# A two-layer graph attention network: sets of seven products that overlap at their ends, and layer 2's gathering one graph later

## The chip, the cores and the metric

The kernel runs on one core of a Trainium2 chip. The metric is the device time of one execution in microseconds (us). TensorE (PE) multiplies, VectorE (DVE) and ScalarE (ACT) do the elementwise work, GpSimd (POOL) issues the accumulating transfers, and SyncE (SP) issues all other DMA transfers. Every engine works through its own instructions in the order in which they stand; engines wait for each other by semaphores.

## The reference

There are 32 graphs of 512 nodes. For each, the input is normalised and rectified, goes through a graph attention layer of 4 heads with 256 features each and an ELU, and then through a second one of 1 head with 512 features; the input is added at the end.

```python
def gat_layer(x, mask, W, a_src, a_dst, bias, concat):
    xl = (x @ W).reshape(B, N, H, F)
    asrc = jnp.einsum('bnhf,hf->bnh', xl, a_src)
    adst = jnp.einsum('bnhf,hf->bnh', xl, a_dst)
    e = jax.nn.leaky_relu(asrc[:, :, None, :] + adst[:, None, :, :], 0.2)
    e = jnp.where(mask[..., None], e, NEG_INF)
    attn = jax.nn.softmax(e, axis=1)
    out = jnp.einsum('bsdh,bshf->bdhf', attn, xl)
    ...
h = jnp.maximum(_layernorm(x, axis=-1), 0.0)
h = jax.nn.elu(gat_layer(h, mask, W1, att_src1, att_dst1, b1, concat=True))
return x + gat_layer(h, mask, W2, att_src2, att_dst2, b2, concat=False)
```

The mask is the adjacency matrix with the diagonal added, and all is fp32.

## The kernel before

**Products.** Most matrix products are cut into 2 x 2 blocks and computed with seven block products in place of eight, with sums of blocks made by DVE beforehand. `sevens` (L866) runs a set of seven for the projections and for layer 2's gathering, `gather1` (L1079) for layer 1's gathering (attention times features), two heads at a time. A product is 8 matmul records for two halves (16 in the second projection). Its sum stands in PSUM. There are four pairs of PSUM banks, given out by `Banks` (L45); a set uses three roles: "a" for products 1, 6, 7 and 4, "b" for 5 and 3, and "g" for 2. Product 1 is copied by ACT from "a" into "g" (the fork), and then 6 goes on accumulating in "a" while 2 goes on in "g". After each product one instruction takes its result out: ACT copies it (`act`, L422) or DVE adds it to what is there (`dve`, L425). So product 6 can start only when the fork copy has read its bank, 7 when the copy of 6 has, and so on; and a new set can start in a bank only when its last result is out. The order of the products is 1, 5, 6, 2, 7, 3, 4 in layer 1's gathering (L1070) and 1, 5, 6, 3, 7, 2, 4 elsewhere (`LAST`, L907). `take2` (L73) gives the free pair to which the narrowest products were last written.

**One graph's turn.** The loop at L1371 runs, on PE and per turn i: gathering of heads 0 and 1 of graph i+1, projection of half the heads of graph i+2, gathering of heads 2 and 3 of graph i+1, projection of the other half of graph i+2, layer 2's gathering of graph i, and the second projection of graph i+1. Each set runs to its end before the next starts. The features of layer 2 stand in one buffer, `xl2`.

**Softmax.** `first` (L710) makes the row sums. For each of four tiles of 128 nodes ACT computes a leaky relu into a buffer `l` (3 of them), DVE adds the mask `mt` and takes the row minimum, and ACT takes the exponential with its sum. Then `spread` (L665) lays the two resulting rows out: DVE transposes them, SP stores them to DRAM (`drr`), and SP loads them broadcast to all partitions (`rr`, two buffers). `second` (L763) makes the attention itself, in buffers `p` (3 of them): DVE combines the row with the column per tile (p<-rr), POOL adds the mask from DRAM by two accumulating transfers (p<-dm), and ACT takes the exponential (p<-p). `columns` (L691) does the same spreading with the row of scores (`das`, `as`).

**Masks and inputs.** `masks` (L555) loads four tiles of the adjacency matrix, makes bf16 masks in `m` (four tiles), stores them to DRAM (`dm`) and has them transposed by two transposing DMAs into `mt`. `norm_turn` (L606) rectifies a tile of x with ACT, stages it as two halves of 16 bit (`adj`<-x), has SP transpose these by DMA (x<-adj, L637), and copies them back into `ht` with ACT. `elu` (L983) uses buffers `xr` (4 of them).

**The order of work.** Every operation is a job with an estimated cost, what it reads and what it writes (`Program`, L87). The PE jobs keep the order in which the program adds them. All other engines' orders are made by a planner (`order`, L234) that simulates the program with its own costs and due times, backwards and forwards, and takes the best of its tries; so a change of a few lines moves instructions on all engines. The whole program has one line per kind of job in the profile: L422 for ACT, L425 for DVE, L428 for SP's transfers, L433 for POOL's, L439 for PE.

Of the kernel before, what the change touches and what calls it, by code (L numbers as in the profile page):

```python
# [44 lines left out]
class Banks:  # L45


    def __init__(self, tiles):
        self.tiles = tiles
        self.free = [(i, j) for i in range(len(tiles)) for j in range(2)]  # L50
        self.written = {q: 512 for q in self.free}

    def take(self, width=512, seeded=0):
        n = [sum(i == k for k, _ in self.free) for i in range(len(self.tiles))]
        fit = [q for q in self.free if self.written[q] >= seeded]
        half = next((q for q in fit if n[q[0]] == 1), fit[0])
        least = min(self.written[q] for q in fit)
        half = next((q for q in fit if self.written[q] == least and n[q[0]] == 1), half)
        self.free.remove(half)
        self.written[half] = max(width, self.written[half] if seeded else 0)  # L60
        i, j = half
        return ("mm", i, j), self.tiles[i][:, j, :]
# [10 lines left out]
    def take2(self, width, seeded=0):  # L73
        whole = [i for i, j in self.free if j == 0 and (i, 1) in self.free]
        least = {i: min(self.written[i, j] for j in range(2)) for i in whole}
        i = min((i for i in whole if least[i] >= seeded), key=least.get)
        self.free = [q for q in self.free if q[0] != i]
        for j in range(2):
            self.written[i, j] = max(width, self.written[i, j] if seeded else 0)
        return [("mm", i, j) for j in range(2)], self.tiles[i]  # L80
# [218 lines left out]
def tile_gat(  # L299
# [79 lines left out]
    xl2 = sbuf.tile([P, NT, DO + 2], F32, name="xl2")  # L379
# [7 lines left out]
    xrs = slots("xr", 4, [P, N])  # L387
    ls = slots("l", 3, [P, N])
    ps_ = slots("p", 3, [P, NT, N])
    m = sbuf.tile([P, NT, N], BF16, name="m")  # L390
# [5 lines left out]
    drs = slots("drr", 2, [2 * NT, P], F32, dram)  # L396
    mds = slots("dm", 3, [P, NT, N], BF16, dram)
    stats = slots("stats", 2, [P, NT, nc.vector.BN_STATS_DIM + nc.vector.BN_AGGR_DIM + 1])
    zs = slots("z", 4, [P, 5, 2, NT])
# [13 lines left out]
    )  # L413

# [140 lines left out]
    def masks(b):  # L555

        for t in range(NT):
            ak, a = adjs.take()
            dma(0.75, (), [ak], a, adj[b, t * P : (t + 1) * P, :])
            dve(  # L560
                0.34, [ak], [("m", t)], nc.vector.tensor_scalar,
                m[:, t, :], a, 0.0, -BIG, op0=OP.is_le, op1=OP.mult,
            )
            adjs.give(ak)
        blocks = bass.AP(tensor=m.tensor, offset=m.offset, ap=[m.ap[0], [N + P, NT], [1, P]])
        every = [("m", t) for t in range(NT)]
        dve(
            0.5, every, every, nc.vector.tensor_max,
            blocks, blocks, diag[:, None, :].to_broadcast([P, NT, P]),
        )  # L570
        MASK[b] = mk, md = mds.take()
        dma(0.45, every, [mk], md.rearrange("p t n -> p (t n)"), m.rearrange("p t n -> p (t n)"))
        tk, mt = mts.take()

        for t in (0, 2):
            prog.add(
                "SP", 1.3, every, [tk + (t // 2,)],
                lambda t=t: nc.sync.dma_start_transpose(
                    mt[:, t : t + 2].rearrange("p t d r -> p (t d) r"),
                    m[:, t : t + 2].rearrange("p t n -> p (t n)"),  # L580
# [76 lines left out]
    class Soft:  # L657
# [7 lines left out]
        def spread(self, v, keys, rows, to, through, n=NT):  # L665

            k = rows * n
            ok, o = to.take()
            dk, dr = through.take()

            c = 32 // k
            sb = o[:, 0, :32]
            dve(
                0.12, keys, [ok], nc.vector.transpose,
                sb, bass.AP(tensor=v.tensor, offset=v.offset, ap=[v.ap[0], [1, k], [0, c]]),
            )
            dma(
                0.03, [ok], [dk], dr[:k].rearrange("k (b j) -> b k j", j=32),
                bass.AP(
                    tensor=sb.tensor, offset=sb.offset, ap=[[c * sb.ap[0][0], P // c], [1, 32]]  # L680
                ),
                0.55,
            )
            dma(
# [6 lines left out]
        def columns(self, i, given=None):  # L691
# [15 lines left out]
                z[:, 0].rearrange("p h t -> p (h t)"), keys, n, ass, das  # L707
            )

        def first(self, h, parts=((0, NT),)):  # L710
# [9 lines left out]
            for d0, d1 in parts:  # L720
# [35 lines left out]
                self.rr[h].append((d0, d1, *self.spread(v, [wk + (2, d0)], 2, rrs, drs, n)))  # L756
# [6 lines left out]
        def second(self, h):  # L763
# [9 lines left out]
            for d0, d1, rk, rr in self.rr.pop(h):  # L773
                at, n, cs = slice(d0 * P, d1 * P), (d1 - d0) * P, range(d0 // 2, d1 // 2)
                long = n == N
                for u in range(NT):
# [7 lines left out]
                    if here:  # L784
                        dve(
                            0.59 if long else 0.34, keys + [("m", u)], keys, nc.vector.tensor_add,
                            p[:, u, at], p[:, u, at], m[:, u, at],
                        )
                rrs.give(rk)
                if not here:  # L790
                    mk, md = MASK[self.b]
                    for us in (0, 1), (2, 3):
                        keys = p_keys(pk, us)
                        accumulate(
                            2.2, keys + [mk], keys,
# [70 lines left out]
    def sevens(left, right, rkeys, put, kh, units, width, order, seeds={}):  # L866
# [3 lines left out]
        for us, n in order:  # L870
            acc, first = ACC[n], n in (1, 5) or n == 2 and us not in forked
            if first:
                seed = seeds.get(n)
                bank[us, acc] = banks.take2(width, 0 if seed is None else M)
# [19 lines left out]
            if n == 1 and banks.able(width):  # L894
                bank[us, "g"] = gks, gt = banks.take2(width, width)
# [11 lines left out]
    LAST = tuple(((0, 1), n) for n in (1, 5, 6, 3, 7, 2, 4))  # L907
    FOUR = LAST + tuple(((2, 3), n) for _, n in LAST)

    PARTS = tuple(((0, 1), n) for n in (1, 2, 5, 6, 3, 7, 4))  # L910
# [4 lines left out]
        (xl2[:, :, :FH], [("xl2", t, 0) for t in range(NT)]),  # L915
        (xl2[:, :, FH + 1 : 2 * FH + 1], [("xl2", t, 1) for t in range(NT)]),
# [45 lines left out]
    def project1(b, left):  # L962
        def to(us, r, c):
# [8 lines left out]
            KQ, [(m, j) for j in range(H // 2) for m in range(2)], W, FOUR,  # L972
# [43 lines left out]
    def sums1(hs_, ps):  # L1016
# [5 lines left out]
        def a_block(i, j):  # L1022
            return (
                xl[:, 2 * j : 2 * j + 2, h0 : h0 + nh, 2 + i * P : 2 + (i + 1) * P],
                [("xl", 2 * j + k, h, i) for k in range(2) for h in hs_],
            )
# [18 lines left out]
        for h, (pk, p) in zip(hs_, ps):  # L1045
# [5 lines left out]
                for r in range(2) for c in range(2)  # L1051
# [18 lines left out]
    PAIRS_OF = tuple(tuple(((h, h + 1), n) for n in (1, 5, 6, 2, 7, 3, 4)) for h in (0, 2))  # L1070
# [8 lines left out]
    def gather1(soft, order):  # L1079

        def some(k, seeded=0):
            if k == 2:
                return banks.take2(M, seeded)
# [7 lines left out]
        for u, n in order:  # L1091
# [3 lines left out]
            if n == 4:  # L1095
                for f in late:
                    f()
            acc, first = ACC[n], n in (1, 5)
            if first:
                bank[u, acc] = some(len(u))  # L1100
# [18 lines left out]
            if n == 1:  # L1119
                bank[u, "g"] = gks, gt = some(len(u), M)  # L1120
# [8 lines left out]
            if n in (5, 6):  # L1129
                over[u] += 1  # L1130
                if over[u] == 2:
# [6 lines left out]
            if n == 4:  # L1138
                for h in u:
                    give_p(soft.p.pop(h)[0])  # L1140
                    yield h

    LATE = 2

    def x2(b):

        if b < B - LATE:
            return xl2

        t = xl if b == B - 1 else w1_sb  # L1150
        return bass.AP(
            tensor=t.tensor, offset=t.offset, ap=[t.ap[0], [DO + 2, NT], [1, DO + 2]]
        )

    def x2_key(b, t, c):
        return ("x2", b, t, c) if b >= B - LATE else ("xl2", t, c)

    def project2(b, left):
        v = x2(b)
        if b >= B - LATE:  # L1160

            if b == B - 1:
                were = [("xl", s, h, i) for s in range(NT) for h in range(H) for i in range(FPH)]
            else:
                were = [k for ix in range(7) for k in w1_keys(ix)]
            for t in range(NT):
                for c in range(2):
                    prog.alias(("x2", b, t, c), were)

        def to(us, r, c):  # L1170
# [7 lines left out]
            lambda n: [("w2", n - 1), ("w2s", n - 1)], minus(to), KH, [(0,), (1,)], W2H, LAST,  # L1178
# [46 lines left out]
    def sums2(b, soft, place=None, keys=None):  # L1225
# [12 lines left out]
        t1, t2, t4 = (  # L1238
            (t.rearrange("p (k f) -> p k f", f=M), [k]) for k, t in (xs.take() for _ in range(3))
# [8 lines left out]
        op(t4, b21, t2)  # L1248
        return left, {1: b11, 2: b21, 3: b22, 4: t4, 5: t1, 6: t2, 7: b12}

    def gather2(b, soft, blocks, order=LAST):
        left, right = blocks
# [3 lines left out]
        def put(n, us, bks, ps, fresh):  # L1256
# [5 lines left out]

            upper[0] -= n in (2, 3)
# [13 lines left out]
        for n in (4, 5, 6):  # L1277
# [28 lines left out]

    def second_layer(b):
# [7 lines left out]
    PLAIN = 0  # L1315
    HT_KEYS = [("ht", t, c) for t in range(NT) for c in range(2)]


    load(0)
# [25 lines left out]
    run(project1(1, left1))  # L1345
# [19 lines left out]
    run(project2(0, left2))  # L1365
# [5 lines left out]
    for i in range(B - 1):  # L1371
        front = i + 2 < B
        s = S1[i + 1]
        last = i == B - 2
        if last:
            for h in gather1(s, SINGLY):
                if h < 2:
                    s.second(h + 2)
                if h == 0:
                    S2[i] = second_layer(i)  # L1380
                if h == 2:
                    S2[i].second(0)
        else:
            run(gather1_plain(s, (0, 1)) if i < PLAIN else gather1(s, PAIRS_OF[0]))
            s.second(2)
            s.second(3)
            S2[i] = second_layer(i)
            S2[i].second(0)
        if front:
            left1 = sums(ht_blocks(), KQ, 0.59)  # L1390
            masks(i + 2)
            ahead = project1(i + 2, left1)
            for _ in range(7):
                next(ahead)
            n = S1[i + 2] = Soft(i + 2, 1, scores_1)
            n.columns(0)
            n.first(0)
            n.first(1)
        if not last:
            run(gather1_plain(s, (2, 3)) if i < PLAIN else gather1(s, PAIRS_OF[1]))  # L1400
        if front:
            run(ahead)
            n.second(0)
            n.second(1)
            n.columns(1)
            n.first(2)
            n.first(3)
        if i < B - 3:
            residual(i)
# [55 lines left out]
```

## Time and profile before

| | |
|---|---|
| Time, median of 3 runs | 2851.67 us (2849.85 to 2853.57) |
| The profiled execution | 2858.08 us, its span 2856.3 us |
| PE busy | 2770.0 us (97%) |
| DVE busy | 2432.2 us (85%) |
| ACT busy | 2384.9 us (83%) |
| DMA queue of SP, share of the 16 engines | 42.5% |
| DMA queue of POOL, share of the 16 engines | 25.6% |
| Granted TensorE clock, mean | 0.993 |

The span runs from the first to the last instruction of one execution. PE's records overlap: a matmul is shown with a modelled end of about 0.38 us after its start while the next one starts 0.216 us after it, so "busy" says where PE had work, and the distance of the starts says how fast it went. "PE mm <- ACT h" means that PE waited and that what ended the wait was an ACT instruction that writes or reads tile h. A bracket behind a row of the timeline gives the idle time before it and its releaser. Tile names have no buffer numbers.

### The profile page before, as it was taken

How to read it: one execution, taken by the hardware profiler on the slowest of the kernel's cores; microseconds unless marked ns; L12 is line 12 of the kernel's file. 1: busy time of each engine (PE TensorE's matmuls, PEld its weight loads, DVE VectorE, ACT ScalarE, POOL GpSimd, SP SyncE). 2: the span in 40 equal slices, each digit the busy share in tenths (PEclk: the TensorE clock that was granted, in tenths of full speed). 3: DMA queues.
4: the chain of work that ended last, by engine and by line, in shares of the span. 5: the costliest groups of instructions: out<-in, count | busy, mean ns of one | idle time of the engine just before them, and what ended most of it. 6: DMA issues, size and time to landing. Idle time of an engine off the chain costs nothing.

```text
span 2856.3 us, 39591 instructions
## 1 busy us (share of the span) xinstructions
PE 2770.0 (97%) x12520; PEld 2373.9 (83%) x12520; DVE 2432.2 (85%) x5494; ACT 2384.9 (83%) x4506; POOL 322.6 (11%) x356
## 2 busy tenths in 40 slices
PE   7999999999999999999999999999999999999988
PEld 6688888888888888888888888888878888888876
DVE  7888898888898878879889888888878988888885
ACT  5888898878898888878888888888878898888882
POOL 0111111101111101111011100111101111111110
PEclk9999999999999999999999999999999999999999
DMA  7666767666777667776687776777666767666652
GB/s 226 153 176 167 204 161 188 181 174 170 189 188 177 176 166 196 167 173 179 172 181 167 196 155 184 170 176 197 164 168 178 195 174 178 183 183 177 176 141 96
DMA packets 369077, 501.42 MB, mean 176 GB/s; under 512 B 220260, under 2 KB 225124, under 8 KB 368868
## 3 DMA queue, kind: packets, MB, share of 16 engines
q1 hardware_dynamic: 323076, 332.15, 42.5%
q0 software_dynamic: 45792, 166.74, 25.6%
q8 instruction: 100, 1.64, 0.2%
q14 instruction: 109, 0.89, 0.1%
HBM read 315.89 MB, written 51.31 MB: 129 GB/s over the span
## 4 chain that ended last, share of the span: by engine, by line
PE 79%; DMA 9%; ACT 5%; DVE 5%; issue 2%; SPq 0%; POOL 0%; ACTq 0%; POOLq 0%; DVEq 0%
PE mm L439 79%; DMA p<-dm 4%; DMA x<-adj 3%; DVE p L425 1%; ACT l L422 1%; ACT p L422 1%; DMA as<-das 1%; ACT adj L422 1%; ACT ht L422 1%; DVE l L425 1%; DVE t L425 1%; DVE hs L425 1%; DVE h L425 1%; ACT xl L422 0%; ACT xr L422 0%
## 5 line engine op out<-in xcount | busy, mean ns | idle before, releaser
L439 PE MATMUL mm<-w_sb,hs 128*128 128x257 f32 (+2 forms) x3032 | 685.3, 383 | 25.1 <-ACT h L422 16.1
L439 PEld LDWEIGHTS mm<-w_sb,hs 128*128 128x128 f32 x3032 | 576.1, 191 | 120.7 <-ACT h L422 20.1
L433 POOL DMA_DIRECT2D p<-dm x314 | 274.4, 878 | 2420.4 <-DVE p L425 1459.7
L422 ACT ACTIVATE l<-l,low 128x512 f32<-128x512 f32 x640 | 455.2, 713 | 40.0 <-DVE low L425 39.3
L439 PE MATMUL mm<-w_sb,ht 128*128 128x258 f32 x2112 | 482.6, 382 | 3.6 <-ACT ht L422 1.4
L425 DVE CUSTOM_DVE_ANT_1 l<-l,mt 128x512 f32<-128x512 f32 x640 | 425.2, 682 | 62.8 <-ACT l L422 62.2
L422 ACT ACTIVATE p<-p,z 128x512 f32<-128x512 f32 (+1 forms) x636 | 424.7, 709 | 62.3 <-DMA p<-dm 51.2
L439 PE MATMUL mm<-p,xl 128*128 128x256 f32 (+1 forms) x1984 | 470.6, 385 | 4.5 <-ACT h L422 3.0
L422 ACT ACTIVATE l<-as,z 128x512 f32<-128x512 f32 x640 | 436.9, 712 | 32.0 <-DMA as<-das 30.7
L439 PE MATMUL mm<-w_sb,h 128*128 128x257 f32 x2056 | 459.5, 380 | 3.3 <-DVE w_sb L425 3.3
L425 DVE SCALAR_TENSOR_TENSOR p<-rr,z 128x512 f32<-128x512 f32 (+1 forms) x636 | 448.1, 740 | 15.8 <-DMA rr<-drr 15.1
L439 PEld LDWEIGHTS mm<-w_sb,ht 128*128 128x128 f32 x2112 | 398.8, 190 | 67.6 <-ACT xl L422 3.3
L439 PEld LDWEIGHTS mm<-w_sb,h 128*128 128x128 f32 x2056 | 390.3, 190 | 62.3 <-DVE w_sb L425 3.7
L439 PEld LDWEIGHTS mm<-p,xl 128*128 128x128 f32 x1984 | 377.8, 191 | 68.0 <-issue 6.9
L422 ACT ACTIVATE xr<-h,b_sb 128x512 f32<-128x512 f32 x248 | 171.8, 714 | 120.9 <-DVE h L425 120.9
L422 ACT ACTIVATE xl<-mm 128x516 f32<-128x516 f32 (+2 forms) x376 | 218.4, 586 | 46.9 <-PE mm L439 45.6
L439 PE MATMUL mm<-t,hs 128*128 128x256 f32 x992 | 233.1, 386 | 25.0 <-ACT mm L422 22.0
L439 PEld LDWEIGHTS mm<-t,hs 128*128 128x128 f32 x992 | 189.7, 193 | 57.5 <-ACT mm L422 27.1
L425 DVE SCALAR_TENSOR_TENSOR h<-h,b_sb,xr 128x512 f32<-128x512 f32 x248 | 181.5, 744 | 46.5 <-ACT xr L422 46.4
L422 ACT ACTIVATE ht<-x 128x1024 uint16<-128x1024 uint16 x120 | 159.3, 1351 | 30.2 <-DMA x<-adj 30.2
L439 PE MATMUL mm<-xl,p 128*128 128x256 f32 (+1 forms) x752 | 180.2, 388 | 2.3 <-DVE t L425 1.6
L422 ACT ACTIVATE h<-mm 128x512 f32<-128x512 f32 (+1 forms) x256 | 146.3, 574 | 26.5 <-PE mm L439 24.4
(113 smaller groups left out, 3268.0 us busy)
## 6 DMA issues: line engine op xcount, KB each, us to landing
p<-dm POOLq DMA_DIRECT2D x314, 512.0 KB, 5.6
rr<-drr SPq DMA_DIRECT2D x159, 512.0 KB
x<-in_x_dram SPq DMA_DIRECT2D x128, 256.0 KB
adj<-in_adj_dram SPq DMA_DIRECT2D x128, 256.0 KB
as<-das SPq DMA_DIRECT2D x64, 512.0 KB
t<-in_x_dram SPq DMA_DIRECT2D x62, 512.0 KB
out_dram<-t SPq DMA_DIRECT2D x60, 512.0 KB
dm<-m SPq DMA_DIRECT2D x32, 512.0 KB
```

The costliest lines, as they stand in the source:

```text
L422: prog.add("ACT", cost, reads, writes, lambda: nc.scalar.activation(*a, **k))
L425: prog.add("DVE", cost, reads, writes, lambda: f(*a, **k))
L433: lambda: nc.gpsimd.dma_start(to, at, accum_op=OP.add), size,
L439: f(*a, **k)
```

## The change

It has four parts.

- **Sets run into each other.** A new function `pipe` takes six of a set's products, and puts the seventh of the set before it behind its own second. `whole`, for the second projection, puts it behind the first. The order of products becomes 1, 5, 6, 2, 3, 7, 4 (the second projection keeps its own, `NEAR`). Banks are given by role: "b" has pair 2, "g" pair 3, and "a" takes pairs 0 and 1 in turn. Two matmuls on the identity write pair 3 at the start. In layer 1's gathering the two row halves of the attention change places, and the last sum of attention blocks is made in place behind product 2.
- **Layer 2's gathering comes one graph later.** In turn i it is that of graph i-1, and `second` for it is placed in the next turn. There are two feature buffers `xl2s`, and the second-to-last graph no longer borrows the space of the first layer's weights.
- **Rows are spread when needed.** `spread` is parted into `lay` (transpose and store, through 4 small buffers `flip` and 8 DRAM rows) and `spread` (the broadcast load), and the load of a row belongs to `second` now.
- **Room.** `xr` has 2 buffers (was 4), `l` 2 (was 3), `m` 2 tiles (was 4), `dm` 4 (was 3), `z` 5 (was 4). Masks are therefore made in halves of two tiles: the second half uses the same `m`. For the last graph the mask is loaded once more from DRAM.

```diff
+    ROLE = {"a": (0, 1), "b": (2,), "g": (3,)}
...
+    def take2(self, role, width, seeded=0):
...
+        own = self.ROLE[role]
+        if role == "a":
+            own = (1 - self.last, self.last)
+        i = next((i for i in own if i in whole), None)
...
-    xl2 = sbuf.tile([P, NT, DO + 2], F32, name="xl2")
+    xl2s = tiles("xl2", 2, [P, NT, DO + 2])
...
-    xrs = slots("xr", 4, [P, N])
-    ls = slots("l", 3, [P, N])
+    xrs = slots("xr", 2, [P, N])
+    ls = slots("l", 2, [P, N])
...
-    m = sbuf.tile([P, NT, N], BF16, name="m")
+    m = sbuf.tile([P, 2, N], BF16, name="m")
+    flips = slots("flip", 4, [P, 32])
...
+        for g in range(2):
+            for t in range(2):
+                ak, a = adjs.take()
+                row = (2 * g + t) * P
+                dma(0.75, (), [ak], a, adj[b, row : row + P, :])
...
+            dma(
+                0.25, every, [mk + (g,)],
+                md[:, 2 * g : 2 * g + 2].rearrange("p t n -> p (t n)"), m.rearrange("p t n -> p (t n)"),
+            )
...
+            flips.give(fk)
+            return dk, dr, rows, n, through
+
+        def spread(self, laid, to):
...
-                self.rr[h].append((d0, d1, *self.spread(v, [wk + (2, d0)], 2, rrs, drs, n)))
+                self.rr[h].append((d0, d1, self.lay(v, [wk + (2, d0)], 2, drs, n)))
...
-            for d0, d1, rk, rr in self.rr.pop(h):
+            for d0, d1, laid in self.rr.pop(h):
+                rk, rr = self.spread(laid, rrs)
...
-    LAST = tuple(((0, 1), n) for n in (1, 5, 6, 3, 7, 2, 4))
-    FOUR = LAST + tuple(((2, 3), n) for _, n in LAST)
+    SEVEN = 1, 5, 6, 2, 3, 7, 4
+    LAST = tuple(((0, 1), n) for n in SEVEN)
+    NEAR = tuple(((0, 1), n) for n in (1, 5, 6, 3, 7, 2, 4))
...
+    behind = []
+
+    def flush():
+        while behind:
+            run(behind.pop())
+
+    def pipe(products):
+
+        for at in range(6):
+            if at == 2:
+                flush()
+            next(products)
+        behind.append(products)
+
+    def whole(products):
+
+        next(products)
+        flush()
+        run(products)
...
+    for i in range(B - 2):
         s = S1[i + 1]
...
+        pipe(gather1(s, PAIRS_OF[0]))
+        left1 = sums(ht_blocks(), KQ, 0.59)
+        pipe(project1(i + 2, left1, 0))
+        s.second(2)
+        s.second(3)
+        if i:
+            S2[i - 1].second(0)
+        S2[i] = second_layer(i)
+        masks(i + 2)
+        pipe(gather1(s, PAIRS_OF[1]))
...
+        pipe(project1(i + 2, left1, 1))
+        n.second(0)
+        n.second(1)
+        if i:
+            residual(i - 1)
+            pipe(gather2(i - 1, S2[i - 1], sums2(i - 1, S2[i - 1])))
         else:
...
+            flush()
...
+        left2 = sums(h1_blocks(), KH, 1.15)
+        whole(project2(i + 1, left2, NEAR))
```

## The prediction

> **What bounds the kernel now.** I read the busy times first, then who TensorE (PE) waits for in the steady part, then two of those waits in the timeline, and last the chain of work.
>
> ```profile
> PE 2770.0 (97%) x12520; PEld 2373.9 (83%) x12520; DVE 2432.2 (85%) x5494; ACT 2384.9 (83%) x4506; POOL 322.6 (11%) x356
> ```
>
> PE is the bound: VectorE (DVE) and ScalarE (ACT) each have over 420 us free. How much could a reordering give? In a dense stretch of the timeline sets of eight matmuls of 256 columns start 1.73 us apart (687.55, 689.28), so one costs 0.216 us. The built program issues 2 records for each of 2604 matmuls of 256 columns, 1800 of 258, 1792 of 257, 48 of 512 and 32 of 128, 3.24 million columns in all, so back to back they would take 3.24 million x 0.216 / 256 = 2734 us. The span is 2856.3: 122 us are not matmul work. 11.8 are before the first matmul and 4 after the last. Going through the starts one by one, and calling lost what two starts are apart beyond that pace, I find about 14 us lost up to 115 us (first graphs), 72 us from 115 to 2740 (the steady part), and 20 us after it (the last graph). The change is about the 72. Who ends these waits:
>
> ```profile
> engine line waited for: us in total, times, longest us
> PE mm L439 <- ACT mm L422: 23.1, 15, 5.4
> PE mm L439 <- ACT h L422: 18.6, 10, 5.6
> PE mm L439 <- DVE t L425: 2.0, 2, 1.2
> PE mm L439 <- ACT xl L422: 1.8, 6, 0.5
> ```
>
> Two releasers hold nearly all, and both are copies out of PSUM by ACT. The first is the copy of product 1 into the fork bank, for which product 6 waits; ten such waits stand in the first set of a graph, right after the second projection. The second is mostly the last copy of that set, for which product 5 of the next set (the projection) waits for a bank; seven times. The worst of each, PE first, then the engine that made it late:
>
> ```profile
> 1711.40 1.89 PE L439 MATMUL mm<-t,hs 128*128 128x256 f32 x8
> 1718.71 3.53 PE L439 MATMUL mm<-t,hs 128*128 128x256 f32 x8 [5.42 <-ACT mm L422]
> ...
> 1714.71 1.33 ACT L422 ACTIVATE p<-p,z 128x512 f32<-128x512 f32 x2 [6.88 <-DMA p<-dm]
> 1715.95 0.58 ACT L422 ACTIVATE xl<-mm 128x514 f32<-128x514 f32 x1
> ...
> 1718.08 0.58 ACT L422 ACTIVATE mm<-mm 128x512 f32<-128x512 f32 x1
> ```
>
> ACT works in order. It stood 6.9 us on an exponential whose accumulating DMA was late, and the 0.58 us copy stood behind it. At 2083.53 the same happens with a transposing DMA:
>
> ```profile
> 1699.80 14.88 DMA p<-dm
> ...
> 2068.13 12.94 DMA x<-adj
> 2083.53 19.37 PE mm L439 x80
> ```
>
> These are lines of the chain of work; the median p<-dm lands in 5.6 us by the list of DMA issues, here it took 14.9 while transposes were in flight. So the steady loss is one of tolerance: how late may ACT, DVE or a DMA be before PE notices? Between a product and the product that needs its bank stands one other product, 1.73 us, less the copy of 0.58.
>
> By starts the 72 us divide into: (a) the ten waits in the first set, 22.7 us and 5.1 us of slow matmuls after them; (b) the seven in the following projection, 17.3 and 3.8; (c) some sixty small ones, none over 1.5 us, 23.2 together.
>
> **The change part by part.** *Sets that overlap, banks by role.* No work is added or removed. The seventh product goes behind the second of the next set, and 2 and 3 stand between 6 and 7. Counted in the two built orders, in PE work between what an instruction needs (itself or what is ahead of it on its engine) and the first product that needs it: copies out of a gathering set go from 1.7 us to 3.5, the last copy of a set to 5.2. All of (c) is covered by one more product of 1.73 us: -23, leaving 1 for luck, so -22.
>
> For (a) and (b) subtract from each wait. With one product more, 16.5 us of waits remain, and three of them still reach 2.8 to 4.1 us, after which matmuls run slowly: 3 x 1.8 = 5.4, in all 22 left. With two products more, 5.9 are left. Which? In the first set of a graph the fork copy keeps one product in half of the cases (nothing is deferred over the second projection), which speaks for none to one. But what is ahead of it on ACT moves: the exponentials of head 1 have 6.9 us in the tightest tenth instead of 4.1, the relu and staging copies of x 6.9 for 3.5, the copies into ht 5.2 for 3.5. That is +2.8, +3.4, +1.7. I take the middle, 14 of 49 left: -35.
>
> The slow matmuls deserve a look. At 1718.71 eight took 3.53 us, where 1.89 is the dense row: 1.6 lost after a wait of 5.4. In this stretch five waits are followed by such a run, 9.0 us in all, one of them a wait of only 2.8. The Trainium skill ("TensorE: Matmul & The Clock Gate", Part 1) says that the clock halves after an idle window of about 3.4 us and comes back after as much work, so 1.7 us for each longer gap: four gaps here, 6.8 us. I use the trace's 9.0, since shorter gaps pay too.
>
> *Gathering one graph later, two buffers.* The layer-2 exponentials, their two accumulating DMAs and the row load get most of a graph's time (about 88 us) more. Work is only moved: per graph 4 DVE of 0.74, 4 ACT of 0.71, 2 POOL issues of 0.86, one row load on SP. It is what makes the room counted above; nothing more is booked. In the last part it comes as extra: the layer-2 softmax of graph 29 now falls beside the singly gathered last graph, where DVE and ACT are 76% busy (2750 to 2790): 0 to +5.8 us. Against it, the wait of 3.3 us at 2745.21 for a sum in the borrowed weight buffer, with 2.1 of slow matmuls, may go, as that buffer is no longer used: -5.4 to 0. I book 0.
>
> *Rows loaded when needed.* Transpose into a small buffer of its own, row load before second instead of after first. SP has the same loads; waiting ones can hold later SP work, but its row loads have in the median 12 to 22 us of PE work of room (before 10 to 21). 0.
>
> *Fewer l, xr and x buffers.* With two l buffers the order leaves fewer than two ACT instructions between the first and second pass of a tile in 38 of 640 tiles (3 before). The DVE pass of 0.68 us is then exposed: 38 x at most 1 = 38 us of ACT waiting, hidden in ACT's 471 idle us; without that cover it is the price. 0.
>
> *Masks in halves.* +32 DVE instructions on half the width (0.41 us for the whole, so at most +13 us in 424 idle), +32 SP issues of 0.34 = 11 us. The real cost is latency: the second half may overwrite the buffer only when the first half's transpose and store have landed. What waits behind it is the first softmax pass of graph i+2, both layer-1 heads. Here a rule speaks against the change: "DMA: Bandwidth & Descriptors" (Anatomy of one DMA) gives each DMA a fixed part of about 2.0 us whatever its size; over 30 graphs that is 60 us if uncovered, as much as all I expect to win. The nearest row, p<-dm at 5.6 us, would give 168. Cover: 13.8 us of PE work in the median stand between these transfers and their first user (before 16.4), more than one landing of 5.6 and 1.3 of issue. I take 0; it is the losing rival.
>
> *Two matmuls on the identity at the start.* At 8 x 0.216 = 1.7 us (twice that if slow) inside the 11.8 us wait for x: hidden. They may spare the sixteen slow transposes there 0.1 us each: -1.7 to 0, I take -1.
>
> **Sum**: -22 - 35 - 1 = -58. The profiled execution took 2858.1 us (span 2856.3 and 1.8 around it), so 2800; the median of the runs is 2851.7, 6.4 below it, so 2794.
>
> **Rivals.** *The waits on late DMAs stay.* DMA engines are 68% busy before and after, transposes and accumulating transfers still meet, and the fork copy after the second projection has half its places no further away. Then only (c) and the start go: -24, so 2828. For it: 14.9 us for a transfer is longer than any room gained. Against: of the 17 waits only five exceed 2.9 us.
>
> *All of it goes*, 72 + 1.7 + 5.4 = 79: 2773, the lower end. The stretch 700 to 1000 shows it possible, with PE busy 299.7 of 300 us.
>
> *Slower: the second mask half arrives too late.* Place: the first passes of heads 0 and 1. It decides from 58 / 30 = 1.9 us per graph uncovered; at half a landing (2.8) it gives 2794 + 84 = 2878. Against: these heads are only needed at the next graph's start, over 40 us later.
>
> *It doesn't matter*: the copies are as late as before because ACT's own DMA waits grow with the room. 2852.
>
> **How the numbers follow.** Likeliest 0.60 (its own range 2776 to 2812), late DMAs stay 0.26, nothing 0.04, slower 0.10. Faster by over 0.2% (5.7 us, about what a measurement of this kernel tells from none) is 0.86. The range runs from all gone (2773) to late DMAs staying with 5.8 more in the last part (2834): 2773 to 2836. Outside are the slower case, half of nothing, and 0.04 on either edge, 0.20.
>
> **What would show it.** Waits on "ACT h" and "ACT mm" in the steady part: under 10 us together for 41.7; slow matmuls nearly gone; PE busy over 98.5%; ACT waiting on p<-dm (51.2) and x<-adj (30.2) still there, but PE no longer behind it. Waits of l on mt's transpose on DVE, or PE waiting on DVE t or hs for several us per graph, would make it wrong.

## The result and the profile after

The changed kernel took 2831.86 us (median of 10 runs, 2817.23 to 2845.99) and the kernel before 2850.39 beside it (10 runs, 2838.96 to 2866.36): 0.9935 of it, 95% interval 0.9907 to 0.9962. That is 18.5 us less; the forecast was 58 less. The profiled execution took 2833.1, its span is 2831.3 (before 2856.3, 25.0 more). The page's line of busy times:

```profile
PE 2765.0 (98%) x12524; PEld 2384.8 (84%) x12524; DVE 2432.6 (86%) x5526; ACT 2389.0 (84%) x4506; POOL 327.3 (12%) x356
```

PE is still the bound, at 97.7%; the prediction wanted over 98.5. Who ends PE's waits from 115 to 2740 us (total, times, longest), as the prediction showed it of before:

```profile
PE mm L459 <- ACT p L442: 17.3, 5, 7.9
PE mm L459 <- ACT mm L442: 9.5, 5, 4.7
PE mm L459 <- DVE t L445: 4.6, 6, 1.8
PE mm L459 <- ACT xl L442: 1.1, 1, 1.1
```

"ACT mm" went from 23.1 to 9.5 and "ACT h" (18.6) is gone from this stretch, as forecast. In their place stands "ACT p", 0.7 us in the whole span of before: PE waits for the attention itself. The longest of these in the timeline, PE first, then ACT:

```profile
1328.43 10.60 PE L459 MATMUL mm<-w_sb,h 128*128 128x257 f32 x48
1346.88 3.78 PE L459 MATMUL mm<-p,xl 128*128 128x256 f32 x8 [7.86 <-ACT p L442]
...
1330.69 1.32 ACT L442 ACTIVATE l<-as,z 128x512 f32<-128x512 f32 x2
1343.14 1.06 ACT L442 ACTIVATE adj<-x 128x1024 uint16<-128x1024 uint16 x1 [11.13 <-DMA x<-adj]
...
1345.52 1.93 ACT L442 ACTIVATE p<-p,z 128x512 f32<-128x512 f32 x3
```

ACT stood 11.1 us on the staging copy of a tile of x, whose buffer an earlier transposing DMA had not yet read. Behind that copy stood the exponentials of head 0, without which the next graph's first set cannot start. Eight matmuls then took 3.78 us instead of 1.89. The wait at 1697.7 (6.8 us) is of the same kind. In the chain of work the accumulating transfers show as before:

```profile
2201.70 15.12 DMA p<-dm
2217.47 0.70 ACT p L442
2218.17 0.95 ACT adj L442
2219.65 89.53 PE mm L459 x404
```

ACT's own waits for these transfers over the whole span, first of before, then after:

```profile
ACT p L422 <- DMA p<-dm: 51.2, 31, 9.8
ACT ht L422 <- DMA x<-adj: 30.2, 9, 8.2
ACT adj L422 <- DMA x<-adj: 6.9, 2, 5.5
```

```profile
ACT p L442 <- DMA p<-dm: 53.1, 44, 5.5
ACT adj L442 <- DMA x<-adj: 23.4, 5, 11.1
ACT ht L442 <- DMA x<-adj: 3.6, 2, 2.1
```

For x<-adj that is 37.1 us before and 27.0 after. The longest single wait moved from the copies into ht, which need the transposed tile, to the staging copies, which need the buffer back.

**Where the 25 us of span came from.** I cut both spans at the same products: the first product of graph 0's second projection, and the end of graph 30's. "Lost" is what lies between the starts of matmuls beyond 0.216 us per 256 columns.

| | head | lost | steady | lost | tail | lost |
|---|---|---|---|---|---|---|
| before | 109.8 | 23.0 | 2640.7 | 79.8 | 105.8 | 19.3 |
| after | 111.8 | 23.3 | 2616.8 | 56.0 | 102.7 | 16.2 |

The steady part gave 24 us. By starts, as in the prediction, it divides so ("long waits" are the prediction's (a) and (b), and after the change the eight waits behind "ACT p" and "ACT mm" in a graph's first set, each with the slow matmuls that follow):

| steady lost, us | before | after | gave | forecast |
|---|---|---|---|---|
| long waits | 49.4 | 39.1 | 10.3 | 35 |
| the stall at 2745.21 for the borrowed weight buffer | 5.2 | 0 | 5.2 | 0 (at most 5.4) |
| the rest, mostly small waits | 25.2 | 16.9 | 8.3 | 22 |

After, the eight waits cost 27.0 us and their slow matmuls 12.1. The two behind the staging copies (1346.88 and 1697.74) alone hold 19.0 of the 39.1.

### The profile page after: what moved, and what is told of

The parts are those of the page before. It is cut to its first block, busy times and chain, and to the rows that moved or that the text cites. A ratio compares the mean times of both kernels' runs of the same rounds, so it can differ in the third digit from the quotient of the medians.

```text
span 2831.3 us, 39738 instructions
## 1 busy us (share of the span) xinstructions
PE 2765.0 (98%) x12524; PEld 2384.8 (84%) x12524; DVE 2432.6 (86%) x5526; ACT 2389.0 (84%) x4506; POOL 327.3 (12%) x356
## 5 line engine op out<-in xcount | busy, mean ns | idle before, releaser
L459 PE MATMUL mm<-w_sb,hs 128*128 128x257 f32 (+2 forms) x3032 | 695.7, 381 | 1.4 <-DVE hs L445 1.3
L459 PE MATMUL mm<-w_sb,ht 128*128 128x258 f32 x2112 | 500.6, 382 | 5.2 <-DVE xl L445 2.4
L459 PE MATMUL mm<-p,xl 128*128 128x256 f32 (+1 forms) x1984 | 485.6, 388 | 20.0 <-ACT p L442 17.5
L442 ACT ACTIVATE l<-l,low 128x512 f32<-128x512 f32 x640 | 455.1, 713 | 39.7 <-DVE low L445 37.9
L442 ACT ACTIVATE p<-p,z 128x512 f32<-128x512 f32 (+1 forms) x636 | 426.9, 709 | 66.8 <-DMA p<-dm 53.1
L442 ACT ACTIVATE xl<-mm 128x514 f32<-128x514 f32 (+2 forms) x380 | 222.5, 586 | 63.4 <-PE mm L459 61.5
L459 PE MATMUL mm<-xl,p 128*128 128x256 f32 (+1 forms) x1024 | 249.2, 386 | 4.7 <-DVE t L445 2.6
L459 PE MATMUL mm<-t,hs 128*128 128x256 f32 x992 | 239.2, 388 | 13.6 <-ACT mm L442 8.8
L459 PEld LDWEIGHTS mm<-t,hs 128*128 128x128 f32 x992 | 191.3, 195 | 45.7 <-ACT mm L442 12.1
L459 PEld LDWEIGHTS mm<-xl,p 128*128 128x128 f32 x1024 | 193.5, 189 | 40.4 <-issue 5.7
L445 DVE TENSOR_TENSOR xl<-xl,mm 128x516 f32<-128x516 f32 (+1 forms) x189 | 129.6, 687 | 48.3 <-PE mm L459 47.0
```

The costliest lines, as they stand in the source:

```text
L442: prog.add("ACT", cost, reads, writes, lambda: nc.scalar.activation(*a, **k))
L445: prog.add("DVE", cost, reads, writes, lambda: f(*a, **k))
L459: f(*a, **k)
```

## The experiments

Where I name a culprit, it is the longest wait of ACT's instructions in the 9 us ahead of a PE wait of at least 0.4 us.

**x transposed by TensorE, in both kernels.** The transposing DMAs of x go; TensorE transposes, ACT's staging copy stays, and the copy out of PSUM is done twice so that ACT has as much to do.

```diff
-        if b < 2:
-            pk, pt = banks.take()
+        if b < B:
+            if b >= 2:
...
+            pk, pt = banks.take(512 if b < 2 else P)
```

> The kernel before with the same edit (x transposed by TensorE, ACT's work kept). Theory 1: the waits of product 6 in the first set (ACT mm, 23 us) and of the following projection (ACT h, 19 us) fall to under 12 together, since both stood behind late p<-dm or x<-adj; time 2850 + 54 - 40 = 2864, and the small waits (23 us) stay. Theory 2: 2850 + 54 = 2904.

> The changed kernel, with x of graphs 2 to 31 transposed by TensorE (16 matmuls on the identity per graph, 1.9 us by the row of graph 1, so 52 to 57 us more PE work in 30 graphs) instead of by DMA; ACT keeps its staging copy and copies the result twice, so its work stays about the same (1.04 + 2 x 0.62 for 1.04 + 1.35). Theory 1 (accumulating DMAs land late because transposing DMAs are in flight, and that is what PE's long waits come from): landings of p<-dm over 9 us fall from 36 to under 12, PE's waits on ACT p and ACT mm (30 us) to under 8, and the time is 2832 + 54 - 35 = 2851. Theory 2 (ACT and DVE have too little room, whatever the DMAs do): the waits stay, 2832 + 54 = 2886.

Before with it: 2917.08 (ratio 1.0209, 1.0176 to 1.0242); changed with it: 2909.91 (1.0182, 1.014 to 1.0223). The 16 transposes of a graph add 16 x 0.108 = 1.7 us, about 52 us over 30 graphs. The first lines of PE's waits, first of before with it, then of the changed kernel with it:

```profile
PE mm L439 <- ACT ht L422: 55.0, 54, 1.3
```

```profile
PE mm L459 <- ACT ht L442: 43.9, 40, 1.3
```

These are new, from the transposes themselves. The old ones are nearly gone: "ACT mm" 1.2 and "ACT h" 3.0 us in before (24.1 and 19.7 over the whole span), "ACT p" 3.0 and "ACT mm" 5.1 in the changed kernel (17.5 and 12.9). The times lie above both theories in both kernels (2864 and 2904 for before, 2851 and 2886 for changed), since neither had booked the new waits. The late transfers differ between the two kernels. Of the 318 accumulating transfers, 23 took over 9 us in before and none without x's transposing DMAs; in the changed kernel 36 did and still 23 without them, where theory 1 wanted under 12. And ACT's waits for p<-dm did not fall with them: 60.9 us in before (51.2), 50.7 in the changed kernel (53.1).

So the old PE waits went when these DMAs went, but that they hung on them is not shown. The edit gave the planner a new order too, and an order alone can do as much, as the last runs show. Also, the transposes and their waits slow PE by over 3 us a graph (52 us and, in before, 55 us over 30 graphs), which gives ACT and DVE that much more time. No run separates these two from the missing DMAs. With the DMAs gone, the two kernels stand 7 us apart.

**No overlap, the changed kernel's order of products kept.** `pipe` and `whole` run their set to its end.

```diff
     def pipe(products):
-        for at in range(6):
...
-        behind.append(products)
+        run(products)
```

> The changed kernel with every set run to its end before the next starts (same product order, same banks by role, layer 2 still one graph later). If the overlap is worth what the prediction booked for small waits and the waits behind the first set: 2832 + 40 = 2872. If the overlap is worth little, because late DMAs decide: 2832 to 2840, with PE's long waits on ACT p and ACT mm as they are.

3003.16 (1.051, 1.047 to 1.055), far above both expectations. Its first waits of PE:

```profile
PE mm L459 <- DVE xl L445: 74.3, 64, 3.5
PE mm L459 <- DVE h L445: 57.0, 61, 1.4
PE mm L459 <- DVE t L445: 26.2, 32, 1.3
```

In the order 1, 5, 6, 2, 3, 7, 4 product 4 goes on in the bank of 7 right behind it, so it waits until DVE has taken 7 out; with the overlap the next set's first two products stand between them. The order needs the overlap. So the fair way to take the overlap away takes the order too:

**No overlap, with the order 1, 5, 6, 2, 7, 3, 4** (`SEVEN`, in all sets but the second projection); **the second layer gathered in its own graph's turn; and both.**

```diff
-    SEVEN = 1, 5, 6, 2, 3, 7, 4
+    SEVEN = 1, 5, 6, 2, 7, 3, 4
```

```diff
-        if i:
-            S2[i - 1].second(0)
         S2[i] = second_layer(i)
+        S2[i].second(0)
...
-            pipe(gather2(i - 1, S2[i - 1], sums2(i - 1, S2[i - 1])))
+            pipe(gather2(i, S2[i], sums2(i, S2[i])))
```

> The changed kernel with no overlap and the order 1, 5, 6, 2, 7, 3, 4 in all sets but the second projection's, that is, the order of before in layer 1's gathering; all else as changed. The run with the order 1, 5, 6, 2, 3, 7, 4 and no overlap lost 165 us to product 4 waiting right behind 7; here 3 stands between them. If the overlap (with its order) carries the gain: 2850 to 2870, as before or slower. If the rest of the change carries it: 2825 to 2838.

> The changed kernel with layer 2's attention and gathering in the same graph's turn again (overlap, buffers, masks in halves, rows when needed as changed). If the deferral gives room: slower than changed, 2845 to 2860, with new waits at the second layer's gathering. If the deferral is what moved accumulating DMAs onto the transposing ones (130 of 318 meet them, 80 before): as fast or faster, 2815 to 2832, with fewer than 100 meeting.

> The changed kernel with both of its headline parts undone: no sets that overlap (every set runs to its end, in the order 1, 5, 6, 2, 7, 3, 4), and the second layer gathered in its own graph's turn. Kept are the banks by role, the rows spread when needed, the masks in halves, the buffers, the sums in place and the swapped halves. Each part alone was worth nothing (2818 and 2828 without one of them, 2832 with both). Theory that the gain lies in what is kept: 2815 to 2832, lost time in the steady part 35 to 50 us. Rival, that either headline part stands in for the other and room is lost only when both go: 2845 to 2858, lost time in the steady part 65 to 80 us, as before the change.

Without the overlap 2817.94 (0.9886, 0.9841 to 0.993); without the later gathering 2828.43 (0.9902, 0.9867 to 0.9936); without either 2846.91 (0.998, 0.9965 to 0.9995). Taking either headline part out cost nothing or gained, taking both out lost nearly all. (Two expectations were met in part only: 103 transfers of the second kernel met transposing DMAs, not under 100, and the third lost 56.6 us in the steady part, between the two forecasts.) I read this as two parts that stand in for each other. The last runs took the ground from that reading: differences of this size come from the order alone.

**A planner told that transposing DMAs take longer** (1.27 and 1.25 us set to 3.0), in three kernels: before, changed, and changed with the gathering in the same turn.

> The kernel before with one number changed twice: the planner takes a transposing DMA to hold the DMA engines for 3.0 us in place of 1.27 (x) and 1.25 (mask). No work is added or removed. If the meeting of transposing and accumulating DMAs costs the time, and a planner that leaves them more time lessens it: landings over 9 us fall from 23 to under 15, time 2815 to 2840. If the planner can't help it: 2845 to 2860.

> The changed kernel with the same two numbers at 3.0 us. If meeting costs the time: landings over 9 us fall from 36 to under 18, PE's waits on ACT p and ACT mm (30 us) to under 12, time 2805 to 2820. If not: 2825 to 2840.

> The changed kernel with layer 2 in the same graph's turn (2828 before this edit) and the same two numbers at 3.0 us. Its landings over 9 us were already 12, so less is left to win: 2810 to 2826. If it is 2805 or below, the deferral costs something that only shows once the DMAs keep apart.

2859.99 (1.0028, 1.0013 to 1.0044), 2854.37 (0.9996, 0.9983 to 1.0009) and 2874.89 (1.0084, 1.0055 to 1.0113). The first is as slow as "the planner can't help it" had it, the other two are slower than either expectation. Landings over 9 us: 23 to 18, 36 to 31 and 12 to 15. In before, ACT's waits for x<-adj fell from 37.1 us to 7.2, but many waits of about 1 us came (17.1 us in 20 for "DVE hs" alone), and the steady loss stayed at 78.0. So these two numbers, set this way, do not help.

**Single parts put into before, and one taken out.** Banks by role (with the two products on the identity); rows spread when needed; and, in the changed kernel without its two headline parts, the rows spread early again.

```diff
-                bank[us, acc] = banks.take2(width, 0 if seed is None else M)
+                bank[us, acc] = banks.take2(acc, width, 0 if seed is None else M)
```

```diff
-                self.rr[h].append((d0, d1, *self.spread(v, [wk + (2, d0)], 2, rrs, drs, n)))
+                self.rr[h].append((d0, d1, self.lay(v, [wk + (2, d0)], 2, drs, n)))
...
+                rk, rr = self.spread(laid, rrs)
```

> The kernel before with one part of the change: the PSUM banks chosen by role, and the two products on the identity at the start that this needs. If the small waits come from which bank is free, they go (23 us in all) and some of the long ones shrink: 2825 to 2835. If banks are not what was short, 2848 to 2856.

> The kernel before with one part of the change: the rows of a head are laid down after the first pass, but spread over the partitions only ahead of the second. If the row loads were in the way of the transposing transfers on SP, or held buffers that the second pass waited for, the waits behind late transfers shrink by a half or more: 2825 to 2838. If they were hidden, as the prediction booked them, 2848 to 2856.

> The changed kernel without overlap and without the later gathering, and also with the rows spread right after the first pass, as before the change. If the rows carry the gain: 2845 to 2856. If they carry nothing: the same as that kernel with rows when needed, within 6 us.

2848.16 (0.9978, 0.9959 to 0.9998), 2854.29 (0.9998, 0.9983 to 1.0014), 2852.19 (0.998, 0.9963 to 0.9997, against 0.998 with the rows late). None carries the gain, in the one order that each was given.

**Nothing changed but the order that the planner finds.** Its assumed cost of the smallest DVE operations is moved by 0.02. TensorE's order stays the same to the last product; 71 to 77% of the places in ACT's queue and 50 to 66% of those in SP's hold another instruction.

```diff
-    COPY, ADD, TINY = 0.28, 0.34, 0.1
+    COPY, ADD, TINY = 0.28, 0.34, 0.12
```

> The kernel before with nothing changed but one number of its planner: the assumed cost of the smallest VectorE operations, 0.12 for 0.1. The built program has the same instructions on TensorE in the same order, but three quarters of ScalarE's queue and half of SP's stand in other places. Theory that the structure (sets, buffers) sets the time: 2850 to 2860, as before. Rival, that which order the planner happens to find decides: it moves by 8 us or more, 2825 to 2847 or above 2863.

> The changed kernel with that one number of the planner changed, 0.12 for 0.1, and nothing else. If structure sets the time: 2827 to 2837, as the changed kernel. If the planner's order decides, 8 us or more away from 2832 on either side, and PE's two long waits behind the staging copies of x (8.0 and 6.8 us) gone or in other places.

> The changed kernel without sets that overlap (order 1, 5, 6, 2, 7, 3, 4, the later gathering kept) with that one number of the planner changed. If structure sets the time: 2813 to 2823, as without the number changed, and below the changed kernel. If the planner's order decides: 2826 or more, no better than the changed kernel.

> The changed kernel with the second layer gathered in its own graph's turn (the overlap kept) with that one number of the planner changed. If structure sets the time: 2823 to 2833. If the planner's order decides: 8 us or more away from 2828 on either side.

And the same number at 0.08:

> The kernel before with the same one number of its planner at 0.08 (0.1 gave 2855, 0.12 gave 2821). If the order found at 0.1 was an unlucky one, with little room behind the transposing transfers of x, this one is faster than it: 2815 to 2840, with ScalarE waiting under 15 us for those transfers (37 us before). If 0.12 was the lucky one: 2848 to 2860, with 25 us or more of these waits.

> The changed kernel with the same one number at 0.08 (0.1 gave 2832, 0.12 gave 2810). If the change itself is worth 10 to 25 us under any order: that much below the kernel before at 0.08, so 2800 to 2825. If its gain is no more than the luck of an order: as slow as that kernel or slower. ScalarE waiting under 15 us for the transposing transfers of x if it comes below 2820 (27 us in the changed kernel as it is).

| planner's number | before | changed | changed / before, by their ratios |
|---|---|---|---|
| 0.08 | 2828.93 (0.9902, 0.9872 to 0.9933) | 2870.63 (1.006, 1.004 to 1.0081) | 1.016 |
| 0.1 | 1 by definition, 2850 to 2859 | 2831.86 (0.9935, 0.9907 to 0.9962) | 0.9935 |
| 0.12 | 2820.94 (0.9856, 0.9834 to 0.9878) | 2810.35 (0.9819, 0.9797 to 0.984) | 0.996 |

Without the overlap 0.12 gave 2808.28 (0.9819, 0.9793 to 0.9846, at 0.1 it was 0.9886), without the later gathering 2836.94 (0.9906, 0.9881 to 0.9931, at 0.1 0.9902). For the two kernels of this document the order theory has it, at both numbers. For the other two it is not settled: the first moved to below both expectations, with intervals that overlap, and the second is where it was by its ratio, though 8.5 us higher by its median. The kernel before, with a planner number moved by 0.02, is faster than the changed kernel; the changed kernel with 0.08 is slower than before. The sign of the change itself goes both ways: 41.7 us more at 0.08 and 10.6 less at 0.12, each pair measured side by side. The two fastest, 2810 and 2808, beat both kernels, but as orders, not as designs.

What the orders do differently can be read in the same two views. Before with 0.12, PE's waits and then ACT's, from 115 to 2740 us:

```profile
PE mm L439 <- ACT mm L422: 18.2, 17, 2.6
PE mm L439 <- ACT h L422: 2.6, 3, 2.0
```

```profile
ACT p L422 <- DMA p<-dm: 49.6, 32, 4.6
ACT ht L422 <- DMA x<-adj: 4.2, 4, 3.2
```

Changed with 0.12, the same two:

```profile
PE mm L459 <- ACT p L442: 13.6, 5, 5.7
PE mm L459 <- ACT mm L442: 1.5, 3, 0.8
```

```profile
ACT adj L442 <- DMA x<-adj: 1.1, 1, 1.1
```

Changed with 0.08, the same two:

```profile
PE mm L459 <- ACT p L442: 31.9, 14, 5.6
PE mm L459 <- ACT mm L442: 8.1, 5, 4.6
```

```profile
ACT p L442 <- DMA p<-dm: 86.1, 67, 3.9
ACT adj L442 <- DMA x<-adj: 29.2, 7, 5.4
```

With 0.12 before lost its "ACT h" (18.6 to 2.6), all PE waits above 2.6 us in this stretch, and 33 us of ACT's waits for x's transposing DMAs; its waits for p<-dm did not shrink (49.6, before 40.4 in this stretch), and 23 transfers took over 9 us, as many as before. The changed kernel with 0.12 lost both waits behind the staging copies. With 0.08 the waits for both kinds of transfer grew. Over the kernels with unpadded planner costs (the times are medians, the last two columns come from the one profiled execution of each, which lay up to 16 us off its median):

| kernel | us | steady lost | ACT on x<-adj |
|---|---|---|---|
| before | 2850 to 2859 | 79.8 | 37.1 |
| before, banks by role | 2848 | 79.5 | 70.7 |
| before, rows when needed | 2854 | 74.8 | 44.9 |
| changed, no headline part | 2847 | 56.6 | 22.6 |
| changed, no headline part, rows early | 2852 | 64.5 | 21.0 |
| changed, 0.08 | 2871 | 80.9 | 32.4 |
| changed | 2832 | 56.0 | 27.0 |
| before, 0.08 / 0.12 | 2829 / 2821 | 43.0 / 43.2 | 2.9 / 4.3 |
| changed, 0.12 | 2810 | 35.3 | 1.5 |
| no overlap, 0.1 / 0.12 | 2818 / 2808 | 39.9 / 37.5 | 8.3 / 1.1 |
| same turn, 0.1 / 0.12 | 2828 / 2837 | 39.1 / 57.6 | 1.4 / 5.5 |

Orders with over 20 us of ACT waits for x<-adj take 2832 to 2871, those with under 10 take 2808 to 2837. It held once as a forecast: the kernel before with 0.08 was to have under 15 us of these waits if it came out fast, and it had 2.9. The culprits agree: of 48.9 us of PE's waits in before's steady part, 19.0 lie behind a wait for x<-adj and 19.2 behind one for p<-dm; with 0.12 it is 1.4 and 17.2 of 26.4. This is a relation over 14 orders, not a cause shown: the padded planner cut these waits to 7.2, 6.0 and 0.6 us, and its three kernels took 2854 to 2875.

## Why the prediction was wrong

**Small waits, -22.** "All of (c) is covered by one more product": 8 came. Many small waits went, but not all: some stayed, waits for "DVE t" grew (2.0 to 4.6 us), and one stall behind them at 142.87 to 149 us holds 4.7 of the 16.9 us left. And since an order alone moves as much, even the 8 can't be put down to the overlap.

**Waits behind late DMAs, -35.** "I take the middle, 14 of 49 left": 39 were left. This is the larger miss, and the step that failed is how the room was counted. I counted PE work between an instruction and its first user in the two built orders, and took the difference as the worth of sets that overlap. The staging copies of x had, by that count, 6.9 us for 3.5, and just these (late by 11.1 and 9.1 us) made the two longest waits, since ACT's queue had head 0's exponentials right behind them. The count doesn't sort the orders either. I count in the built programs the PE work between the last product that a transposing DMA of x has to await and the first that has to await it, through the queues too, and take the tightest of a graph's four. The median over the graphs is 12.1 us in before and 12.1 in it with 0.12, which is 1.4% faster; it is 15.6 in the changed kernel, 13.8 in it with 0.12, and 15.6 with 0.08, which is the slowest of all. The count says how much work stands between, not when a transfer lands or what a late one holds up. What was to show the step fell with it: the rows of slow matmuls went from 10.9 to 15.5 us in the steady part instead of nearly vanishing, and ACT still waits on p<-dm and x<-adj, as said, but with PE behind it. What makes a given transfer late stays open.

**The structure as the cause.** Under both terms lies the assumption that the difference between two built programs belongs to what the diff says. Moving one assumed cost spreads the kernel before over 1.4% and the changed one over 2.4%, by the ratios, about 40 and 70 us. Of the 18.5 us I can therefore assign none to the overlap, the later gathering, the banks or the rows. That the time fell at all is in part luck of the order: at 0.08 the changed kernel is slower than the kernel before. What the change is worth over many orders stays open: three pairs, +1.6%, -0.65% and -0.4%, can't tell it.

**The terms booked at 0, and the start.** Masks in halves: DVE waited for a transposed mask, in the view of its waits over the whole span,

```profile
DVE l L445 <- DMA mt<-m: 2.2, 4, 0.8
```

2.2 us in all, and no PE wait named it. So the losing rival fell in this order, and with it the case for adding the 2.0 us fixed part of a DMA ("DMA: Bandwidth & Descriptors", Anatomy of one DMA in the Trainium skill) thirty times. That section fits its figure to transfers issued by GpSimd, and the mask transfers are SP's; no run here times the fixed part. What the trace shows is that it was covered, as the 13.8 us of PE work counted ahead of the first user had it. Fewer l buffers: ACT waiting for DVE's low, 39.3 before, 37.9 after. Both held. The start was to give 1 and took 2.0 (head 109.8 to 111.8): PE's wait for x fell from 11.8 to 7.7, but the first products did not come sooner. The last part gave 3.1 where 0 was booked, and the stall at 2745, which the prediction counted there as well, the 5.2 above.

**The sum:** -10.3 - 8.3 - 5.2 + 2.0 - 3.1 = -24.9, the 25.0 between the spans but for rounding; the medians differ by 18.5.

**The rivals.** "The waits on late DMAs stay", 2828, was 4 us off and had 0.26. Its reason, that a transfer can take longer than any room gained, fits the trace after, where one took 16.2 us. Its sum is near by luck: it gave the long waits nothing and the small ones all their 23, where 10 and 8 came. Against it I had set that only five of 17 waits exceeded 2.9 us, which says how late transfers were in one order, not how late they can be. The range held the time.

**The slow matmuls.** The prediction counted four gaps over 3.4 us, for the rule of an idle window, and five rows of slow matmuls. They are not the same places: the gap of 3.68 us at 242.18 was followed by no slow matmuls (granted clock 1.00 from 242 to 247 us), those of 2.68 us at 588.07 and 3.10 us at 1010.77 were. After the change a wait of 1.76 us at 145.73, 2.9 us behind one of 0.86, was enough (granted clock 0.53 from 145.7 to 149.3 us). So shorter gaps cost time too, as the prediction said.

## What to carry to other kernels

Where a planner orders the queues, run two or three null changes of its costs on both kernels before any gain below their spread is put down to a design. Read the culprit behind each wait of the bound engine: the releaser that the profile names is often only the last in a queue, and a change can empty one name and fill another. Trying several orders of one design on the chip can be worth more than a redesign: one number gave 1.2% to the changed kernel and 1.4% to the one before, where the redesign gave 0.65%.

## What the runs showed of the hardware

The latest accumulating transfers (512 KB, from POOL) are those in company of transposing DMAs. Counting the transfers in whose flight over 100 transposing packets start against the rest: in before 80 against 238, median landing 7.2 against 5.2 us, longest 15.2 against 9.4; in the changed kernel 130 against 188, 7.0 against 6.0, longest 16.2 against 9.8; in it with 0.08, 119 against 199, 7.5 against 6.3, longest 19.6 against 9.9. Over the profiles of all 20 kernels here, each of the 89 transfers that took over 12 us met that many, and none of the others took over 11.6. Without x's transposing DMAs none took over 12 in either kernel (4 did in before, 8 in the changed kernel). Two things speak for caution. A transfer that is late for another reason has more time to meet packets, and the medians are not always apart that way: in the changed kernel without the overlap, those that met took 5.5 us and the rest 6.0. How many are late does not set the time either: 23 took over 9 us in before, and 23 in it with 0.12, which took 0.9856 of its time.

One program is spread widely from execution to execution: before took 2833.5 to 2871.2 in 71 runs of one comparison, the changed kernel 2817 to 2846 in 10. Why is open.
